# A graph layer on one core: the order of the edges is asked at the end of the program instead of by a branch at its beginning

## The chip, the cores and the metric

The kernel runs on one core of a Trainium2 chip. A core has a matrix engine (TensorE, "PE" in the profile; its weight loads are "PEld"), a vector engine (VectorE, "DVE"), a scalar engine (ScalarE, "ACT"), a general engine (GpSimd, "POOL") and a sync engine (SyncE, "SP") that here only issues transfers. Each engine works through its own queue in order. Transfers run on 16 DMA engines and are issued from the queues of SP, ACT and POOL. The metric is device time in microseconds (us), the median of several runs; lower is better.

## The reference

There are 6250 nodes with 256 numbers each (`x`) and 100000 edges `src -> dst`, which the inputs bring sorted by `dst`.

```python
theta_x = (x[dst] - x[src]) @ theta_w.T + theta_b
phi_x = x[src] @ phi_w.T + phi_b
e = relu(theta_x + phi_x)
out = segment_max(e, dst, num_segments=6250)      # 0 where a node has no edge
return layernorm(x + out)                          # eps 1e-5, no scale, no shift
```

Since `x[dst]` is the same for all edges of a node, the kernel takes the maximum over `b = x @ (phi_w - theta_w).T` of the source nodes first, and adds `x @ theta_w.T` and the biases of the node itself behind it.

## The kernel before

The program is one long list of instructions with no loop on the chip. It is written in program order; a scheduler then orders each engine's queue by when it reckons an instruction can start, program order first among those that are ready, so an instruction may be issued well ahead of its place in the text. Only the inside of a conditional block can't be mixed with what is outside it. The nodes are split: part 1 (the first 1130) is done from gathered rows alone, part 2 (the last 5120, 40 tiles of 128) mostly by selection matmuls.

**Beginning (L528 to L661).** SP loads `src_1`, ACT's queue loads `dst_i` and `dst_1` and copies both edge lists to `src_list` and `dst_list` in DRAM. L602 and L604 count the places where `dst` falls (`n_descents`), and `add_up` (L575: a matmul with ones and a copy) writes the count to `flags[0]`. `search_edges` (L621) finds for each partition where its window of 800 edges ends (`window`) and gathers that window (`dst_w`, `src_w`) on POOL. L652 loads the count into a register of every engine, and L653 branches: with a count over 0, a bitonic sort (`sort_edges`, L123) rewrites both lists, and the loads, the first gathers and the search are done again. With these inputs the count is 0 and the block is jumped over.

**Preparation (L710 to L784).** SP loads the weights (`w_in`, L719) and biases (L722); PE transposes the weights (L739). Twelve shares of up to four tiles of x (`x_q`, L775) and six groups of eight gathered rows (`x_group`, L764) are transposed by PE (L747), copied by ACT (L749), multiplied (L759) and copied out (L762); the shares go to `b_rows` in DRAM. The pools of this stage are closed at its end, and the tiles of the fetch stage below (`rows`, `raw`, `terms`, `want`, `hot`) are laid out behind that.

**Table and choice (L929 to L1031).** On DVE, `fill_table` spreads the window over a table of 40 nodes by 36 ranks (L938 to L979), and `choice` picks, for each of 17 blocks of source rows (slots), at most one edge per node (L1004 to L1022). `wanted` (L1024) transposes the choice and stores it to `chosen_rows`.

**Fetch (`slot_part`, L1056).** There are 85 parts: 17 slots by 5 blocks of 1024 nodes. A part loads its `want` row (L1061), builds three one-hot matrices (`hot`: two ACT passes each, L1067 and L1068; later the first by one DVE instruction, L1065), and PE multiplies them with the slot's rows in two terms (L1075, 24 matmuls). ACT copies the result of slot 0 (L1084), DVE takes the maximum for the others (L1086, twice per part). `terms` (L1053, L1054) are made once per slot.

**Runs of gathered rows.** POOL gathers rows with `gather` (L515; the DMA is issued in L512, and short `pause` instructions of L488 space the gathers out). DVE runs a capped maximum over them (L688), and SP stores them (L696). First 48 gathers of x, then 98 of `b_rows` (part 1), then the edges that no slot took: `list_pieces` (L1167 to L1235, DVE) compacts them, and 232 gathers by `list_src` fetch their rows (part 2). All POOL gathers are chained in program order (`in_turn`, L506).

**End (L1319 to L1344, L1454).** Shares of up to eight tiles: gather of the maxima (`place_1`, `place_2`), PE for `x @ theta_w.T`, DVE sum and ReLU, ACT for the variance (L1328) and the normalisation (L1338), store (L1344). Then all columns of `bad` (conditions under which the fast way does not hold) are added up, and L1461 branches to `general_path` if there was any; here it is jumped over.

Of the kernel before, what the change touches and what calls it, by code (L numbers as in the profile page):

```python
# [40 lines left out]
FP = mybir.dt.float32  # L41
# [6 lines left out]
ALU = mybir.AluOpType  # L48
# [4 lines left out]
P = 128  # L53
# [50 lines left out]
def load_rows(queue, t, src, total):  # L104

    n_rows, width = t.shape
    whole, rest = min(divmod(total, width), (n_rows, 0))
    queue.dma_start(t[:whole, :], flat(src, 0, [[width, whole], [1, width]]))
    if rest:
        queue.dma_start(t[whole : whole + 1, :rest], flat(src, whole * width, [[width, 1], [1, rest]]))  # L110


def load_chunks(queue, t, dst, steps, total):


    queue.dma_start(t[1 : P - 1, :], flat(dst, steps - 1, [[steps, P - 2], [1, steps + 2]]))
    queue.dma_start(t[0:1, 1:], flat(dst, 0, [[steps, 1], [1, steps + 1]]))
    first = (P - 1) * steps - 1
    n = min(total - first, steps + 2)
    queue.dma_start(t[P - 1 : P, :n], flat(dst, first, [[steps, 1], [1, n]]))  # L120


def sort_edges(nc, pool, psum, src, dst, src_sorted, dst_sorted, ident):  # L123

    n_edges = src.shape[0]
    width = 1 << (SORT_BITS - 7)
    n_blocks = width // P

    d = pool.tile([P, width], I32, name="sort_dst")
    s = pool.tile([P, width], I32, name="sort_src")
    nc.vector.memset(d, ID_MASK)
    nc.vector.memset(s, 0)
    load_rows(nc.sync, d, dst, n_edges)
    load_rows(nc.scalar, s, src, n_edges)


    index = pool.tile([P, width], I32, name="sort_index")
    nc.gpsimd.iota(index, pattern=[[1, width]], base=0, channel_multiplier=width)  # L140
    gray = pool.tile([P, width], I32, name="sort_gray")
    nc.vector.tensor_scalar(gray, index, 1, None, op0=ALU.logical_shift_right)
    nc.vector.tensor_tensor(gray, gray, index, op=ALU.bitwise_xor)

    keys = [pool.tile([P, width], FP, name=f"keys{i}") for i in range(2)]
    first = keys[0].bitcast(I32)
    nc.vector.tensor_scalar(d, d, ID_BITS, KEY_OFFSET, op0=ALU.logical_shift_left, op1=ALU.bitwise_or)
    nc.vector.tensor_tensor(first, d, s, op=ALU.bitwise_or)
    at = 0

    def compare(distance):
        nonlocal at
        a, b = (k.rearrange("p (a two b) -> p a two b", two=2, b=distance) for k in (keys[at], keys[1 - at]))
        nc.vector.tensor_tensor(b[:, :, 0, :], a[:, :, 0, :], a[:, :, 1, :], op=ALU.min)
        nc.vector.tensor_tensor(b[:, :, 1, :], a[:, :, 0, :], a[:, :, 1, :], op=ALU.max)
        at = 1 - at

    def transpose():

        nonlocal at  # L160
        ps = psum.tile([P, n_blocks, P], FP, name="sort_ps")
        for c in range(n_blocks):
            nc.tensor.transpose(ps[:, c, :], keys[at][:, c * P : (c + 1) * P], ident)
        nc.vector.tensor_copy(keys[1 - at], ps.rearrange("p c f -> p (c f)"))
        at = 1 - at

    flips = pool.tile([P, width], I32, name="sort_flips")
    for k in range(1, SORT_BITS + 1):
        bits, bit = (index, 1) if k == 1 else (gray, k - 1)
        nc.vector.tensor_scalar(  # L170
            flips, bits, 31 - bit, -(1 << 31), op0=ALU.logical_shift_left, op1=ALU.bitwise_and
        )
        now = keys[at].bitcast(I32)
        nc.vector.tensor_tensor(now, now, flips, op=ALU.bitwise_xor)
        j = k - 1
        if (1 << j) >= width:
            transpose()
            while (1 << j) >= width:
                compare((1 << j) // width)
                j -= 1  # L180
            transpose()
        while j >= 0:
            compare(1 << j)
            j -= 1

    done = keys[at].bitcast(I32)
    nc.vector.tensor_scalar(d, done, ID_BITS, ID_MASK, op0=ALU.logical_shift_right, op1=ALU.bitwise_and)
    nc.vector.tensor_scalar(s, done, ID_MASK, None, op0=ALU.bitwise_and)
    nc.sync.dma_start(flat(dst_sorted, 0, [[width, P], [1, width]]), d)
    nc.scalar.dma_start(flat(src_sorted, 0, [[width, P], [1, width]]), s)  # L190
# [237 lines left out]
def gnn_kernel(ctx: ExitStack, tc: tile.TileContext, x, src, dst, theta_w, theta_b, phi_w, phi_b, out):  # L428
# [106 lines left out]
    def gather_group(i, table, a=0, b=STEPS):  # L535
        t0, n = groups[i]
        if i not in ring_tiles:
            ring_tiles[i] = gathered.tile([P, STEPS, D], FP, name="g")
        return [
            gather(ring_tiles[i][:, k, :], table, src_1[:, t0 + k : t0 + k + 1]) for k in range(a, min(b, n))  # L540
        ]
# [33 lines left out]
    def add_up(per_partition, to):  # L575
        ps = misc()[0:1, 0:1]
        nc.tensor.matmul(ps, per_partition, ones, start=True, stop=True)
        nc.vector.tensor_copy(to, ps)
# [17 lines left out]
    nc.vector.memset(list_pads, PAD_WORD)  # L596
    nc.sync.dma_start(flat(list_words, 0, [[OWN_LIST, 1], [1, OWN_LIST]]), list_pads[:1, :])
    nc.sync.dma_start(flat(list_words, (P + 1) * OWN_LIST, [[OWN_LIST, 3], [1, OWN_LIST]]), list_pads[:3, :])
    bad = const.tile([P, 9], FP, name="bad")

    descents = search.tile([P, T + 1], FP, name="descents")
    nc.vector.tensor_tensor(descents, dst_i[:, : T + 1], dst_i[:, 1:], op=ALU.is_gt)  # L602
    n_descents = search.tile([P, 1], FP, name="n_descents")
    nc.vector.tensor_reduce(n_descents, descents, AX.X, ALU.add)  # L604
    add_up(n_descents, flags[:, 0:1])

# [12 lines left out]
    def search_edges():  # L621

        nc.vector.tensor_copy(ids[:, : T + 1], dst_i[:, 1:])
        iota(ids[:, T + 1 :], 0, 0, T)
        nc.vector.tensor_copy(low0, ids[:, 0:1])
        nc.vector.memset(low0[0:1, :], -1.0)
        nc.vector.tensor_scalar(last_node, first_node, TILES - 1.0, None, op0=ALU.add)
        nc.vector.tensor_scalar(hot0, columns[:, 2, :], low0, None, op0=ALU.is_ge)
        nc.vector.scalar_tensor_tensor(hot0, columns[:, 2, :], ids[:, T : T + 1], hot0, op0=ALU.is_lt, op1=ALU.mult)
        cut = 2 * D  # L630
        for i, (a, b, n) in enumerate(((cut, T + 2, T), (0, cut, cut))):
            pp = misc()
            nc.tensor.matmul(pp[:, : b - a], hot0, ids[:, a:b], start=True, stop=True)
            nc.vector.tensor_scalar(
                descents[:, a:n], pp[:, : n - a], last_node, None, op0=ALU.is_le, op1=ALU.add, accum_out=counts[:, i : i + 1]
            )
            nc.vector.tensor_tensor(end, counts[:, i : i + 1], end if i else pp[:, T + 1 - a : T + 2 - a], op=ALU.add)

        nc.vector.tensor_scalar(counts[:, 0:1], end, -float(WINDOW), 0.0, op0=ALU.add, op1=ALU.max)
        nc.vector.tensor_scalar(window, counts[:, 0:1], float(E - WINDOW), None, op0=ALU.min)  # L640
        nc.vector.tensor_scalar(bad[:, 0:1], end, float(WINDOW), None, op0=ALU.is_lt)
        gather_run(dst_w, dst_list, window)
        gather_run(src_w, src_list, window)

    search_edges()
    gather_group(of_x[0], x, EARLY_STEPS)

    with (
        tc.tile_pool(name="sort", bufs=1) as sort,
        tc.tile_pool(name="ps_sort", bufs=2, space=PSUM) as ps_sort,  # L650
    ):
        n_unsorted = nc.values_load(flags[0:1, 0:1])  # L652
        with tc.If(n_unsorted > 0):  # L653
            sort_edges(nc, sort, ps_sort, src, dst, src_list, dst_list, ident)
            load_chunks(nc.sync, dst_i, dst_list, T, EDGES)
            load_chunks(nc.sync, dst_1, dst_list, T1, EDGES)
            load_rows(nc.scalar, src_1, src_list, P * T1)
            latest[0] = None
            gather_group(of_x[0], x)
            search_edges()  # L660
    latest[0] = None  # L661
    early.close()
    for i in of_x[1:]:
        gather_group(i, x)
# [168 lines left out]
    def last_or_none(to, last_place, has, none):  # L833
        nc.vector.scalar_tensor_tensor(last_place, last_place, float(-none), has, op0=ALU.add, op1=ALU.mult)
        nc.vector.tensor_scalar(last_place, last_place, float(none), float(none), op0=ALU.add, op1=ALU.min)
        nc.vector.tensor_copy(to, last_place)

    def places_1():
        has = work.tile([P, NT1], FP, name="has_1")
# [615 lines left out]
    n_bad = const.tile([P, 1], FP, name="n_bad")  # L1455
    nc.vector.tensor_reduce(n_bad, bad, AX.X, ALU.add)
    add_up(n_bad, flags[:, 1:2])
    body.close()

    n_over = nc.values_load(flags[0:1, 1:2])  # L1460
    with tc.If(n_over > 0):  # L1461
        general_path(tc, x, theta_w, pick, bias_terms, out, b_rows, src_list, dst_list, ident, E)


# [22 lines left out]
```

## Time and profile before

| what | us |
| --- | --- |
| median of 3 runs | 749.13 (747.54 to 750.01) |
| the profiled execution | 746.02 |
| span of its instructions | 744.2 |
| PE busy | 650.4 (87%) |
| DVE busy | 641.4 (86%) |
| POOL busy | 604.9 (81%) |
| ACT busy | 492.7 (66%) |
| the 1960 matmuls of L1075 | 458.0 |

The page divides the span into 40 slices of 18.6 us and gives each engine's busy share in tenths; PEclk is the clock granted to TensorE, in the same tenths. Further views used are the list of waits (who waited for whom: total us, times, longest), the timeline (start us, duration us, engine, line, operation, and in brackets the idle time before it with what ended it), the stretches (busy time of each engine between two times) and the chain of waits that ended last.

### The profile page before, as it was taken

The page shows a single profiled execution, that of the slowest core. Times are in us where ns is not written, and L with a number is a line of the kernel's source. Part 1 is how long each engine was busy: PE and PEld are TensorE (multiplying, and loading weights), DVE is VectorE, ACT ScalarE, POOL GpSimd, SP SyncE. Part 2 cuts the span into 40 slices and gives each one's busy share as a digit, 9 for nine tenths or more (in the row PEclk, how much of TensorE's full clock was granted, in tenths as well). Part 3 has the DMA queues.
Part 4 walks back from the last instruction along what each step waited for, and adds up shares of the span by engine and source line. Part 5 has one row for each costly group of instructions (what it writes and reads, how often), then busy time and mean ns, then how long its engine had stood idle before and what let it go on. Part 6 is the DMA issues. An engine that isn't in the chain of part 4 may idle for free.

```text
span 744.2 us, 10255 instructions
## 1 busy us (share of the span) xinstructions
PE 650.4 (87%) x3018; PEld 537.3 (72%) x3018; DVE 641.4 (86%) x1197; ACT 492.7 (66%) x700; POOL 604.9 (81%) x843
## 2 busy tenths in 40 slices
PE   1299999939777999999999999999999999589970
PEld 0288888726556788688888888888888888479970
DVE  6699999999997989598889989889799899768871
ACT  0144444459997777688777877877787775037885
POOL 7788987788887778888888888888888888648840
PEclk9599999959999999999999999999999999999995
DMA  6577745584677787968777777768768777625542
GB/s 207 144 244 244 248 159 193 176 286 151 209 239 256 239 254 231 356 211 267 230 235 223 261 243 251 228 223 251 262 205 261 229 222 250 224 101 180 180 173 116
DMA packets 55895, 164.84 MB, mean 221 GB/s; under 512 B 11835, under 2 KB 19796, under 8 KB 48500
## 3 DMA queue, kind: packets, MB, share of 16 engines
q1 hardware_dynamic: 32344, 98.76, 38.1%
q0 software_dynamic: 20944, 57.62, 27.5%
q10 hardware_dynamic: 2540, 7.69, 2.9%
q8 instruction: 27, 0.44, 0.3%
q14 instruction: 40, 0.33, 0.1%
HBM read 101.08 MB, written 63.74 MB: 221 GB/s over the span
## 4 chain that ended last, share of the span: by engine, by line
PE 52%; ACT 11%; DVE 5%; DMA 5%; POOL 3%; issue 2%; DVEq 0%; ACTq 0%; POOLq 0%; SPq 0%
PE ps_f L1075 49%; DMA want<-chosen_rows 4%; POOL g L512 3%; ACT x_f L1338 3%; ACT squares L1328 3%; ACT hot L1067 2%; ACT hot L1068 2%; DVE acc L1086 2%; PE ps_e L1299 1%; ACT acc L1084 1%; DMA g<-b_rows,src 1%; ACT x_t L1294 1%; DVE g L688 1%; DVE x_f L1314 1%; DVE g L1310 0%
## 5 line engine op out<-in xcount | busy, mean ns | idle before, releaser
L1075 PE MATMUL ps_f<-hot,terms 128*128 128x512 f32 x1960 | 458.0, 395 | 29.0 <-ACT hot L1068 15.6
L1075 PEld LDWEIGHTS ps_f<-hot,terms 128*128 128x128 f32 x1960 | 370.2, 190 | 113.1 <-ACT hot L1068 19.8
L512 POOL DMA_INDIRECT g<-b_rows,list_src x232 | 235.4, 1015 | 39.4 <-issue 35.6
L1067 ACT ACTIVATE hot<-want,minus_row 128x1024 fp32r<-128x1024 f16 x169 | 186.2, 1147 | 92.7 <-PE ps_f L1075 80.2
L1086 DVE TENSOR_TENSOR acc<-acc,ps_f 128x1024 f32<-128x1024 f32 x160 | 193.5, 1215 | 31.9 <-PE ps_f L1075 31.0
L688 DVE SCALAR_TENSOR_TENSOR g<-g,caps 128x256 f32<-128x256 f32 x376 | 180.0, 479 | 8.4 <-DMA g<-b_rows,src 5.2
L1068 ACT ACTIVATE hot<-hot 128x1024 fp32r<-128x1024 f32 x169 | 169.1, 1046 | 0.0
L512 POOL DMA_INDIRECT g<-b_rows,src x98 | 128.0, 1306 | 30.5 <-issue 25.3
L488 POOL IOTA pause<- 128x160 f32 x384 | 120.4, 314 | 5.5
L759 PE MATMUL ps_b<-weights,x_t 128*128 128x256 f32 x388 | 90.5, 388 | 1.3 <-ACT x_t L749 0.5
L759 PEld LDWEIGHTS ps_b<-weights,x_t 128*128 128x128 f32 x388 | 72.9, 192 | 14.4 <-ACT x_t L749 5.0
L512 POOL DMA_INDIRECT g<-in_x_dram,src x48 | 60.3, 1256 | 11.3 <-issue 7.1
L512 POOL DMA_INDIRECT g<-maxima,place x49 | 47.6, 972 | 24.6 <-issue 22.5
L1065 DVE TENSOR_SCALAR hot<-want,row_id 128x1024 fp32r<-128x1024 f16 x76 | 59.8, 788 | 6.4 <-DMA want<-chosen_rows 6.3
L1299 PE MATMUL ps_e<-weights,x_t 128*128 128x256 f32 x192 | 48.5, 380 | 0.3 <-ACT x_t L1294 0.2
L1299 PEld LDWEIGHTS ps_e<-weights,x_t 128*128 128x128 f32 x192 | 32.8, 190 | 3.9 <-ACT x_t L1294 0.8
L1294 ACT COPY x_t<-ps_e 128x512 f32<-128x512 f32 x24 | 13.7, 574 | 32.4 <-PE ps_e L1292 32.4
L762 ACT COPY b_sb<-ps_b 128x512 f32<-128x512 f32 (+1 forms) x25 | 14.4, 578 | 29.8 <-PE ps_b L759 28.0
L762 ACT COPY g<-ps_b 128x512 f32<-128x512 f32 x24 | 14.1, 586 | 29.8 <-PE ps_b L759 27.5
L1338 ACT ACTIVATE x_f<-x_f,r 128x256 f32<-128x256 f32 x49 | 25.3, 590 | 10.8 <-DVE r L1335 10.7
L749 ACT COPY x_t<-ps_xt 128x512 f32<-128x512 f32 (+1 forms) x49 | 26.1, 593 | 0.0
L1328 ACT ACTIVATE squares<-x_f,r 128x256 bf16<-128x256 f32 x49 | 24.2, 499 | 1.6 <-DMA g<-b_rows,list_src 1.0
(266 smaller groups left out, 502.2 us busy)
## 6 DMA issues: line engine op xcount, KB each, us to landing
maxima<-g SPq DMA_DIRECT2D x47, 1024.0 KB
want<-chosen_rows SPq DMA_DIRECT2D x85, 256.0 KB
x_q<-in_x_dram SPq DMA_DIRECT2D x12, 512.0 KB
b_rows<-b_sb ACTq DMA_DIRECT2D x12, 512.0 KB
x_f<-in_x_dram SPq DMA_DIRECT2D x5, 1024.0 KB
out_dram<-x_f SPq DMA_DIRECT2D x5, 1024.0 KB
raw<-b_rows SPq DMA_DIRECT2D x16, 256.0 KB
g<-b_rows,list_src POOLq DMA_INDIRECT x232, 4.3
```

Of the source, the lines that this page charges most:

```text
L488: return nc.gpsimd.iota(t, pattern=[[step, t.shape[1]]], base=base, channel_multiplier=per_partition, allow_small_or_imprecise_dtypes=True,)
L512: in_turn(nc.gpsimd.indirect_dma_start(out=out, out_offset=out_offset, in_=in_, in_offset=in_offset))
L688: one = nc.vector.scalar_tensor_tensor(g[:, k, :], last[part], caps[:, t : t + 1], g[:, k, :], op0=ALU.min, op1=ALU.max)
L759: nc.tensor.matmul(ps[:, h, :], x_t[:, h, k, :], weights[:, k, 0, :], start=(k == 0), stop=(k == KC - 1))
L1065: nc.vector.tensor_scalar(hot[:, b, :], want, row_id[:, b : b + 1], None, op0=ALU.is_equal)
L1067: nc.scalar.activation(hot[:, b, :], want, AF.Abs, bias=minus_row[:, b : b + 1], scale=1.0)
L1068: nc.scalar.activation(hot[:, b, :], hot[:, b, :].bitcast(FP), AF.Relu, bias=1.0, scale=-1.0)
L1075: nc.tensor.matmul(ps[:, w : w + 512], terms[:, part, b, h * P : (h + 1) * P], hot[:, b, w : w + 512], start=(i == 0), stop=(i == n - 1),)
L1086: latest_part[0] = nc.vector.tensor_tensor(to, to, ps, op=ALU.max).ins.name
L1299: nc.tensor.matmul(a[:, i, :], x_t[:, 2 * i + c, :], weights[:, c, 1, :], start=(c == 0), stop=False)
L1328: nc.scalar.activation(squares, x_f[:, k, :], AF.Square, bias=mean[:, k : k + 1], scale=1.0, accum_out=var[:, k : k + 1])
L1338: nc.scalar.activation(x_f[:, k, :], x_f[:, k, :], AF.Identity, bias=mean[:, k : k + 1], scale=inv[:, k : k + 1])
```

## The change

The count of falls is no longer read at the beginning. It becomes a tenth column of `bad`, so that unsorted edges lead into the conditional block at the end, and `flags[0]` is written there. The sort stands inside that block, in an inner conditional of its own, ahead of the general path, which then runs on the sorted lists. The repeated loads, gathers and search fall away. Because the fast way now also runs over unsorted edges, one place index is kept from falling below 0.

```diff
-    bad = const.tile([P, 9], FP, name="bad")
+    bad = const.tile([P, 10], FP, name="bad")
...
-    n_descents = search.tile([P, 1], FP, name="n_descents")
+    n_descents = bad[:, 9:10]
     nc.vector.tensor_reduce(n_descents, descents, AX.X, ALU.add)
-    add_up(n_descents, flags[:, 0:1])
...
     search_edges()
     gather_group(of_x[0], x, EARLY_STEPS)
-
-    with (
-        tc.tile_pool(name="sort", bufs=1) as sort,
-        tc.tile_pool(name="ps_sort", bufs=2, space=PSUM) as ps_sort,
-    ):
-        n_unsorted = nc.values_load(flags[0:1, 0:1])
-        with tc.If(n_unsorted > 0):
-            sort_edges(nc, sort, ps_sort, src, dst, src_list, dst_list, ident)
-            load_chunks(nc.sync, dst_i, dst_list, T, EDGES)
-            load_chunks(nc.sync, dst_1, dst_list, T1, EDGES)
-            load_rows(nc.scalar, src_1, src_list, P * T1)
-            latest[0] = None
-            gather_group(of_x[0], x)
-            search_edges()
-    latest[0] = None
     early.close()
...
-        nc.vector.tensor_copy(to, last_place)
+        nc.vector.tensor_scalar(to, last_place, 0.0, None, op0=ALU.max)
...
     add_up(n_bad, flags[:, 1:2])
+    add_up(n_descents, flags[:, 0:1])
     body.close()
 
     n_over = nc.values_load(flags[0:1, 1:2])
     with tc.If(n_over > 0):
+        n_unsorted = nc.values_load(flags[0:1, 0:1])
+        with (
+            tc.tile_pool(name="sort", bufs=1) as sort,
+            tc.tile_pool(name="ps_sort", bufs=2, space=PSUM) as ps_sort,
+            tc.If(n_unsorted > 0),
+        ):
+            sort_edges(nc, sort, ps_sort, src, dst, src_list, dst_list, ident)
         general_path(tc, x, theta_w, pick, bias_terms, out, b_rows, src_list, dst_list, ident, E)
```

## The prediction

> **What bounds the kernel now.** I read the 40 slices first, then the chain, then the stretches and waits at both ends of it.
>
> ```profile
> PE   1299999939777999999999999999999999589970
> DVE  6699999999997989598889989889799899768871
> ```
>
> PE stands still in the first 30 us and works with gaps from slice 9 to 14 (about 150 to 280 us). DVE is full from slice 3 on.
>
> ```profile
> 150.00:200.00 50.00, 33.69 (x121) 24.68 (x121) 48.99 (x85) 41.21 (x67) 43.12 (x28) 0.80 0.68 219
> 400.00:500.00 100.00, 100.00 (x442) 82.79 (x442) 89.44 (x130) 77.86 (x78) 88.94 (x133) 1.00 0.75 238
> 311.66 309.57 PE ps_f L1075 x1364
> ```
>
> The first two lines are stretches (busy us, with counts in brackets, of PE, PEld, DVE, ACT, POOL; granted clock; DMA), the third is the chain's longest piece. From 311 us to 621 us PE is busy without a break on the fetch matmuls, so every microsecond of fetch done before that comes off the end, if nothing else holds the end. What else holds it is POOL:
>
> ```profile
> 277.18 1.14 POOL L512 DMA_INDIRECT g<-b_rows,list_src  x1 [1.79 <-DVE caps L1235]
> 660.81 0.95 POOL L512 DMA_INDIRECT g<-maxima,place  x1 [15.07 <-issue]
> ```
>
> POOL gathers from 277 us to 645.5 us with no idle time but about 0.2 us of issue per gather, then waits 15.07 us for the last maxima to be stored. So the end has two supports: PE's fetch, and POOL with 15.07 us to spare.
>
> **The beginning.**
>
> ```profile
> PE ps_xt L739 <- DMA biases<-in_L_gnn_phi_b_dram: 15.4, 1, 15.4
> DVE ids L669 <- DVEq L653: 4.0, 1, 4.0
> POOL g L512 <- DMA src_w<-src_list,window: 2.5, 1, 2.5
> SPq L719 <- POOLq L653: 3.5, 1, 3.5
> ...
> L653 SPq COMPARE_BRANCH  x1: 45/45/45, 10.2 to 10.2; - x1
> L653 POOLq COMPARE_BRANCH  x1: 53/53/53, 24.5 to 24.5; - x1
> ...
> 25.02 0.39 SPq L719 DMA_DIRECT2D w_in<-in_L_gnn_phi_w_dram  x1
> 34.23 2.65 PE L747 MATMUL ps_xt<-ident,x_q 128*128 128x128 f32 x10
> ```
>
> SP is at the branch at 10.2 us, POOL, behind its gathers, only at 24.5 us; SP's load of the weights waits for that and goes out at 25.02 us. PE transposes the first x tile at 34.23 us, although the first x tiles were asked for at 3.75 us. The weights wait and the x tiles don't, presumably because w_in's place is one that a sort tile had. A third place shows where the preparation's end is waited for:
>
> ```profile
> 148.16 0.26 ACT L1030 CAST rows<-ps 80x128 f16<-80x128 f32 x1
> 161.94 2.19 ACT L1067 ACTIVATE hot<-want,minus_row 128x1024 fp32r<-128x1024 f16 x2
> ```
>
> The first choice was transposed by PE at 95.75 us, but is copied out only at 148.16 us, right behind the last copy of the preparation (147.68 us), whose space it takes over; the first one-hot follows at 161.94 us.
>
> **The change, part by part.**
>
> (1) *Weights.* Without the branch SP can issue w_in where it now issues x_q (3.75 us) or before it. Landing took 5.8 us (25.02 to 30.8). From 4 to 14 us the DMA engines are 0.83 to 1.02 busy at about 300 GB/s, so the 0.77 MB of weights and biases cost some 2.6 us there. 3.75 + 5.8 + 2.6 = 12.1, plus 3.4 us for the weight transposes (30.8 to 34.2): x at about 15 us. If the weights go out first, at about 1 us, it is 10 us; with a slip of 2 to 3 us on SP's queue, 17. I take 14, which is 20 us earlier, between 17 and 24. The same 0.77 MB could delay the window's lists by 0 to 2.6 us; I take 0, since the DMA engines are only 0.02 busy at 16 to 18 us, before the window is gathered at 18.01 us.
>
> (2) *Preparation.* From 36 to 100 us PE is over 98% busy, so it is its own limit and ends 20 us earlier, at 128 us. It needs the x gathers: POOL's last is issued at 109.6 us, the change takes 2.5 us off (4), and a gather lands in 3.9 us, so they are there at 111; the last group takes PE 7 us, from 121. They don't hold it.
>
> (3) *Fetch begins.* The 14.3 us from 147.68 to 161.94 (clearing raw, slot loads, want) I keep. ACT is then the limit (25.00 of 25 us in 200 to 225). This stretch shifts by the 20 us.
>
> (4) *POOL.* The branch cost POOL the 2.5 us of idle time above. The list gathers at 277.18 us had waited 1.79 us for DVE; DVE's list work comes earlier (5), so they start at 277.2 - 2.5 - 1.8 = 272.9, 4.3 us earlier. At the end POOL could then go on 15.07 + 4.3 = 19 us earlier: the most that this support allows.
>
> (5) *DVE.* It idles from 17.7 to 25.8 us but for 0.24 us. Fifteen groups of small work on weights, biases and caps now lie behind 25.8 us in the table's way: by their rows 0.16 + 0.22 + 0.68 + 0.42 + 0.27 + 0.41 + 0.44 + 0.47 + 4 x 0.41 for L726 to L740 and 1.6 for L673 to L806 make 6.3 us. They can move into that idle time. So choice and list work end about 6 us earlier, 0 to 6.3.
>
> (6) *How much of PE's 20 us stays.* A part that is not of slot 0 costs DVE 2 x 1.21 + 0.75 = 3.2 us and PE 24 x 0.234 = 5.6 us. DVE is full from 150 to 225 us, so parts done earlier need DVE time: the 6.3 us, and 7.9 us idle from 225 to 277 (44.12 of 52.00 busy), of which 5.2 us are waits for gathers (L688) and may stay. 6.3 + 2.7 = 9.0 us give 2.8 parts, 16 us of PE; all 14.2 us give 4.4 parts, 25 us. Slot 0's five parts are copied by ACT, so the low end is safer than it looks. I take 16, the case where the gather waits stay, between 6 and 20.
>
> (7) *The end.* The second add_up is two passes of 0.19 us in all on PE and 0.14 us on DVE (L577, L578), at about 635 us, where PE waits 2.6 us for a one-hot; uncovered, 0.35 us. The extra max takes the copy's place (L836, 0.17 us; its neighbour L835, two operations, 0.38): 0.2 us, before a 1.03 us wait of DVE; uncovered, 0.2. What the branch jumps over gets longer; there it is the same jump, and the trace bounds it: DVE's branch is at 736.6 us and its next event at 739.4, so -0 to +2.8 us; I take 0, since the target was not near before either. Five loads of the count (0.5 us each) and five branches vanish inside (1) and (4).
>
> On (7), the Trainium skill (Runtime: NRT & Kernel Launch, Instruction fetch mechanics) says that a taken branch to a target outside the window loaded must first fetch the target's page; by that rule a longer block costs the same one fetch, so 0, and if every jump cost a second fetch, the sum would be 736 instead of 733. The trace's 3.1 us on DVE at L653 (18.2 to 21.3) agrees with a fetch.
>
> Sum: PE 16, POOL 19, the smaller counts. 744.2 - 16 = 728; with 1.8 us around the span 730 against 746.0 for that execution. This lies 3.1 us under the median of 749.13, so in the metric I forecast **733 us**.
>
> **The rivals.**
>
> *A, the forecast: fetch moves ahead.* 12 to 20 us off: 729 to 737. For it: PE's idle start, its full stretch, POOL's 15 us. Chance 0.50.
>
> *B, DVE or POOL holds the lead back.* DVE's order stays as it is, parts gain only its 6.3 us, or the end follows POOL's 4.3 us because its last wait is not free: 743 to 745. For it: DVE's 48.99 of 50; against it: L1086 can fill DVE's waits. Chance 0.24. The Trainium skill (SBUF — State Buffer, Who interferes with whom) lets a DVE operation in a two-port mode shut POOL out altogether. By it the 0.75 us of L1065 for 4.4 earlier parts would cost POOL 3.3 us, leaving POOL 15.7 and the sum near 733; the gathers of 206 to 276 us, with L1065 among them, take 1.08 us against 0.95 at best, so the trace shows little of it.
>
> *C, more than forecast:* the 14.3 us of (3) shrink too, and POOL's 19 us or more come off: 725 to 729. Chance 0.08.
>
> *D, it doesn't do what it says:* another dependence still keeps the weights back, only POOL's 2.5 us go: 747 to 749. Against it: the row names L653. Chance 0.07.
>
> *E, slower.* The earlier fetch puts L1086 and L1054 ahead of the list work in DVE's queue, and the list gathers, behind which POOL has an unbroken row to 645 us, start later. Each part ahead costs 3.2 us, less the 6.3. It decides once they start later than 277 + 15 = 292, that is from seven parts on ((15.07 + 6.3) / 3.2). With all nine parts that the choice loop holds: 9 x 3.2 - 6.3 - 15.1 = 7.4 us lost, 756. For it: those parts come first in program order; against it: ACT needs 6.6 us for a part's three one-hots, so only three or four fit into the 20 us. Chance 0.11.
>
> **How the numbers follow.** A, B and C are faster by over 0.3% (2.2 us, about what a measurement can tell from no change): 0.82. D is 0.07 the same, E 0.11 slower. The predicted time is A's. The range leaves out D, E and the extremes of C: 725 to 746.
>
> **What would show it.** Weights issued by SP before 10 us and x transposed by 17; the last copy of L762 at about 128 instead of 147.68; the first L1067 at about 142; choice (L1022) and L1235 some 6 us earlier; the first list gather at about 273; PE unbroken from before 311; the wait before the last gathers (15.07) down to a few us. Wrong it would be if L1075 starts early but the list gathers start after 277 (E), or if the weights go out late (D).

## The result and the profile after

The kernel after took 752.26 us (median of 20 runs, 749.96 to 757.0) against 749.21 for the one before (20 runs, 743.11 to 755.5): ratio 1.0054, 95% interval 1.0032 to 1.0076. A later pair of measurements gave 752.03 against 750.18, ratio 1.0031 (0.9997 to 1.0065). The profiled span went from 744.2 to 751.2 us. But the profiled execution of before (746.02) was 3.2 us faster than the median of its runs, and that of after (752.98) 0.7 us slower: 3.9 of these 7.0 us are scatter of single executions, and the medians differ by 3.05. The forecast was 733, so the change came out on the other side.

From L653 on, a line of before has a number lower by 16 in after (L688 is now L672). The slices of PE and DVE after:

```profile
PE   1999999277379799989999999999999999589980
DVE  6499999997799979779979889889889899768881
```

PE does start early now, in the second slice, and has a new hole in the eighth (131 to 150 us). DVE has a seven in five slices between the 10th and the 20th (10, 11, 15, 17, 18); before it had one seven (13) and one five (17) there. The stretches (busy us and counts of PE, PEld, DVE, ACT, POOL; granted clock; DMA), of after:

```profile
125.00:150.00 25.00, 11.68 (x54) 8.86 (x52) 24.19 (x62) 6.64 (x21) 19.81 (x18) 0.77 0.66 219
150.00:200.00 50.00, 35.38 (x135) 26.00 (x133) 43.17 (x92) 48.28 (x69) 41.29 (x33) 0.87 0.71 235
200.00:250.00 50.00, 33.82 (x133) 26.30 (x134) 45.28 (x77) 36.07 (x52) 41.30 (x31) 0.84 0.62 195
```

and of before, the two that were not shown:

```profile
125.00:150.00 25.00, 22.13 (x115) 18.62 (x113) 24.41 (x64) 11.19 (x22) 19.95 (x17) 1.00 0.60 202
200.00:250.00 50.00, 39.04 (x161) 29.36 (x161) 44.37 (x94) 43.25 (x66) 39.64 (x35) 0.97 0.78 246
```

Up to 125 us PE was busy 107.5 us after and 95.4 before: a lead of 12.1 us. In 125 to 150 it loses 10.5 of it and in 200 to 250 another 5.2, where it also runs at a granted clock of 0.84 instead of 0.97. DVE did 5.8 us less work in 150 to 200 (43.17 against 48.99). From 400 to 500 us PE is busy throughout in both (100.00 us).

Waiting is only a part of what PE lost. The page's rows for the fetch matmuls (busy us, mean ns of one; then the idle time before them), of before and of after:

```profile
L1075 PE MATMUL ps_f<-hot,terms 128*128 128x512 f32 x1960 | 458.0, 395 | 29.0 <-ACT hot L1068 15.6
L1059 PE MATMUL ps_f<-hot,terms 128*128 128x512 f32 x1960 | 464.0, 398 | 39.5 <-DVE hot L1049 13.4
```

The same 1960 matmuls take 6.0 us more. Most take 0.39 us; 29 of them took over 0.6 us in before and 53 in after, and these stand in groups behind PE's waits, where the granted clock is low (0.50 from 139 to 162 us in after). From the start to the end of the last fetch matmul, all 2602 matmuls together kept PE busy 583.2 us in before and 587.2 in after, and PE stood idle for 69.4 and 72.6 us. So of the 7.2 us by which the last fetch matmul came later, 4.0 are longer busy time (the fetch matmuls 6.0 more, the others 2.0 less) and 3.2 are added waiting.

Now the beginning, in after's waits of the first 35 us (us in total, times, longest):

```profile
POOL dst_w L512 <- DVE window L639: 7.8, 1, 7.8
PE ps_xt L723 <- DVE weights L724: 6.4, 1, 6.4
DVE w_in L718 <- DMA w_in<-in_L_gnn_theta_w_dram: 2.5, 1, 2.5
DVE ids L653 <- DMA dst<-in_dst_dram: 2.4, 1, 2.4
DVE bias L710 <- DMA biases<-in_L_gnn_phi_b_dram: 2.1, 1, 2.1
```

and the same in the order of time, SP, DVE, PE and POOL (start, us, instruction, idle time before it and its releaser):

```profile
1.19 0.42 SPq L703 DMA_DIRECT2D w_in<-in_L_gnn_phi_w_dram  x1
6.97 0.69 DVE L718 TENSOR_TENSOR w_in<-w_in 128x512 f32<-128x512 f32 x1 [2.50 <-DMA w_in<-in_L_gnn_theta_w_dram]
...
13.13 1.72 DVE L711 CAST high_part<-bias 128x256 fp32r<-128x256 f32 x1
...
24.91 0.15 DVE L639 TENSOR_SCALAR window<-counts 128x1 int32<-128x1 f32 x1
17.71 1.20 PE L731 MATMUL ps_xt<-ident,x_q 128*128 128x128 f32 x3 [1.26 <-DVE weights L724]
25.33 0.96 POOL L512 DMA_INDIRECT dst_w<-dst_list,window  x1 [7.83 <-DVE window L639]
```

The weights go out at 1.19 us and x is transposed at 17.71. But weights, biases and the chunk ids now stand *in front of the search* in DVE's queue, and DVE stands still for each of their loads; the window is ready at 24.91 us instead of 17.59. The middle and the end, on ACT and POOL:

```profile
135.25 0.26 ACT L1014 CAST rows<-ps 80x128 f16<-80x128 f32 x1
153.49 1.16 ACT L1051 ACTIVATE hot<-want,minus_row 128x1024 fp32r<-128x1024 f16 x1
...
287.21 1.02 POOL L512 DMA_INDIRECT g<-b_rows,list_src  x1 [0.30 <-issue]
667.96 0.95 POOL L512 DMA_INDIRECT g<-maxima,place  x1 [11.43 <-issue]
```

The preparation ends 12.9 us earlier (135.25 against 148.16), the fetch begins 8.5 us earlier (153.49 against 161.94), and the list gathers start 10 us *later* (287.21 against 277.18). Between the first two lies this, on DVE:

```profile
143.12 0.40 DVE L988 TENSOR_SCALAR wide<-padded 128x960 int16<-128x960 int16 x1
143.63 0.70 DVE L1019 MEMSET raw<- 128x768 f32 x1
144.25 0.36 DVE L672 SCALAR_TENSOR_TENSOR g<-g,caps 128x256 f32<-128x256 f32 x1
144.53 0.27 DVE L806 TENSOR_SCALAR hot<-columns,low 128x128 f32<-128x128 f32 x1
...
168.84 0.65 DVE L1006 TENSOR_TENSOR unused<-unused,wide 128x960 int16<-128x960 int16 x1
...
189.73 0.49 DVE L672 SCALAR_TENSOR_TENSOR g<-g,caps 128x256 f32<-128x256 f32 x1 [4.41 <-DMA g<-b_rows,src]
```

Line 988 begins a new round of the choice, and it is broken off: raw's memset and node_place's one-hots (L806), with runs (L672) between them, come first. Before, the same instructions stood behind the whole choice, whose last instruction is L1022:

```profile
149.70 0.66 DVE L1022 TENSOR_TENSOR unused<-unused,wide 128x960 int16<-128x960 int16 x1
...
152.55 0.70 DVE L1035 MEMSET raw<- 128x768 f32 x1
```

Before, the choice ended at 150.36 us. After, it ends at 169.49 (L1006), and the runs have got so far ahead (79 by 170 us, 62 before) that they wait for the rows that POOL gathers: 9.8 us in 150 to 260, against 5.2 before. What comes behind them in DVE's queue waits too: PE had to wait 8.1 us for one slot's terms (L1038).

### The profile page after: what moved, and what is told of

Same layout as the page of the kernel before. It is cut to its first block, busy times and chain, and to the rows that moved or that the text cites. A ratio compares the mean times of both kernels' runs of the same rounds, so it can differ in the third digit from the quotient of the medians.

```text
span 751.2 us, 10220 instructions
## 1 busy us (share of the span) xinstructions
PE 654.4 (87%) x3018; PEld 539.9 (72%) x3018; DVE 639.7 (85%) x1197; ACT 493.1 (66%) x700; POOL 606.7 (81%) x843
## 4 chain that ended last, share of the span: by engine, by line
PE 40%; DVE 12%; DMA 9%; POOL 8%; ACT 8%; issue 4%; DVEq 0%; SPq 0%; ACTq 0%; POOLq 0%
PE ps_f L1059 37%; POOL g L512 6%; DMA want<-chosen_rows 4%; ACT x_f L1322 3%; DVE acc L1070 3%; DMA g<-b_rows,src 3%; ACT squares L1312 3%; DVE g L672 2%; PE ps_e L1283 1%; POOL pause L488 1%; DMA g<-b_rows,list_src 1%; ACT hot L1051 1%; DVE work L1187 1%; DMA raw<-b_rows 1%; DVE hot L1049 1%
## 5 line engine op out<-in xcount | busy, mean ns | idle before, releaser
L1059 PE MATMUL ps_f<-hot,terms 128*128 128x512 f32 x1960 | 464.0, 398 | 39.5 <-DVE hot L1049 13.4
L672 DVE SCALAR_TENSOR_TENSOR g<-g,caps 128x256 f32<-128x256 f32 x376 | 180.2, 479 | 12.8 <-DMA g<-b_rows,src 9.8
L1052 ACT ACTIVATE hot<-hot 128x1024 fp32r<-128x1024 f32 x169 | 169.0, 1046 | 0.0
L512 POOL DMA_INDIRECT g<-in_x_dram,src x48 | 61.9, 1289 | 9.1 <-issue 7.1
L1322 ACT ACTIVATE x_f<-x_f,r 128x256 f32<-128x256 f32 x49 | 25.3, 589 | 10.6 <-DVE r L1319 10.5
```

Of the source, the lines that this page charges most:

```text
L512: in_turn(nc.gpsimd.indirect_dma_start(out=out, out_offset=out_offset, in_=in_, in_offset=in_offset))
L672: one = nc.vector.scalar_tensor_tensor(g[:, k, :], last[part], caps[:, t : t + 1], g[:, k, :], op0=ALU.min, op1=ALU.max)
L1052: nc.scalar.activation(hot[:, b, :], hot[:, b, :].bitcast(FP), AF.Relu, bias=1.0, scale=-1.0)
L1059: nc.tensor.matmul(ps[:, w : w + 512], terms[:, part, b, h * P : (h + 1) * P], hot[:, b, w : w + 512], start=(i == 0), stop=(i == n - 1),)
L1322: nc.scalar.activation(x_f[:, k, :], x_f[:, k, :], AF.Identity, bias=mean[:, k : k + 1], scale=inv[:, k : k + 1])
```

## The experiments

Three theories stood against each other. *B*: the window, 7.3 us late, is carried to the end. *M2*: the loss is DVE's order in the middle. *P*: the end is set by PE's fetch, and the list gathers matter little. Besides these, *M* says only that the earlier preparation is to blame, *N* that it is the code moved to the end or the missing branch.

The chips differed. On three of five (marked s; the other two are called quiet) the kernels stood still at several places, for up to 26.6 us at once. From the last fetch matmul to the end of the span the profiles there show 118 to 122 us, where the quiet ones of the table show 91.0 to 91.6, and before took 816 to 825 us there instead of 749 to 753. Such a stop in the first run of hold_weights, as the profile's waits show it:

```profile
DVE acc L1081 <- remote: 29.0, 4, 26.6
```

There times are compared only with before on the same chip, and what the trace tells is read ahead of the first long stop; in before_shift1, hold_shift1 and raw_apart_2 shorter ones, of up to 4.8 us, lie ahead of what is read.

| kernel | ratio to before (95%) | window | preparation ends | choice ends | first list gather | last fetch matmul | span |
|---|---|---|---|---|---|---|---|
| before | 1 | 17.6 | 148.3 | 150.4 | 277.2 | 652.6 | 744.2 |
| after | 1.0054 (1.0032 to 1.0076) | 24.9 | 135.3 | 169.5 | 287.2 | 659.8 | 751.2 |
| after_again | 1.0031 (0.9997 to 1.0065) | 25.1 | 134.6 | 169.0 | 286.8 | 657.6 | 749.0 |
| hold_weights_3 | 1.0057 (1.0019 to 1.0095) | 18.0 | 148.0 | 149.5 | 287.3 | 664.2 | 755.3 |
| search_first_3 | 1.0003 (0.9977 to 1.0029) | 16.6 | 145.7 | 163.2 | 279.3 | 659.0 | 750.0 |
| choice_ahead_2 | 0.9993 (0.9964 to 1.0021) | 25.4 | 133.7 | 157.8 | 281.7 | 655.0 | 746.4 |
| choice_search_2 | 0.9989 (0.9957 to 1.0021) | 16.6 | 147.1 | 153.0 | 282.5 | 658.2 | 749.5 |

Starts and ends in us, each from the one profiled execution of its kernel. The two profiles of after differ by 0.8 us at most up to the first list gather, but by 2.2 us at the last fetch matmul. The profiles also come from different chips, and some lie well off their kernel's median: before's 3.2 us under it, choice_ahead_2's 3.4 us. So a few microseconds in the last two columns decide nothing; the ratios do, and of these the last four are from one chip, on which after itself was not timed.

**after_again**, no edit.

> The kernel after, unchanged, on the chip of the study, beside before. If the loss is the same there as at first: ratio 1.003 to 1.008, window at 25 us, last copy of the preparation at 135, choice ended at 169, first list gather at 287. If the chip's state adds stalls that neither kernel had at first, the ratio may lie anywhere between 0.98 and 1.02; then only the stretches ahead of the first such stall are compared between kernels.

As expected; a quiet chip.

**hold_weights, hold_weights_2, hold_weights_3**: the change without its earlier preparation. The load of w_in waits for the window's gather, and SP's other loads of the preparation stand behind it.

```diff
+                tc.add_manual_dep(load.ins, window_read[0], landed, reason="after the window")
...
+            behind_in_order(one, held, "after the window")
```

> The kernel after, with the loads of w_in, biases and x_q held behind the landing of the window's dst_w gather: no branch, but the preparation starts when it did with the branch. Theory M (all of the loss comes from the preparation being earlier): the window at about 17.6 us, the last copy of the preparation at 145 to 148, choice ended by 152, the first list gather at 275 to 279, the last fetch matmul at 650 to 654, ratio to before 0.994 to 1.001. Rival N (the work put at the end, or the branch's absence itself, costs the 4 us): the middle is back as said, but the ratio stays at 1.003 to 1.010, and the stretch behind the last fetch matmul is longer than before's 92 us.

> The kernel of hold_weights once more: no branch, the preparation as late as before. Theory M (the earlier preparation causes the loss): window at 17 us, choice ended by 151, first list gather at 272 to 279, last fetch matmul 648 to 654, ratio 0.992 to 1.001. Theory N (the work at the end, or the code without the branch, costs it): the middle as before, ratio 1.003 to 1.010.

> The kernel of hold_weights again, on a chip without the stalls of the earlier two looks. Theory M (the earlier preparation causes the loss): window at 17 us, choice ended by 151, last COPY_PREDICATED at 213 to 226, first list gather at 272 to 280, last fetch matmul 648 to 654, ratio 0.992 to 1.001. Theory N (the work at the end, or the code without the branch, costs it): the middle as before, ratio 1.003 to 1.010.

The runs on s chips gave 1.0064 (1.0017 to 1.0112) and 0.9970 (0.9868 to 1.0073), the quiet one 1.0057. N's first half falls: from the last fetch matmul to the end of the span it is 91.0 us here, 91.4 in after, 91.6 in before, so the code moved to the end costs nothing. M falls as the only cause: window, preparation and choice are where before has them, and yet the list gathers come at 287 us and the kernel is slow. N's other half, that the missing branch alone costs something by another way, is not excluded: this kernel has no branch either, its beginning is where before has it, and it is slow. POOL's gathers (start, us) in hold_weights_3:

```profile
180.33 7.69 POOL L512 DMA_INDIRECT g<-b_rows,src  x1 [0.30 <-issue]
188.32 9.49 POOL L512 DMA_INDIRECT g<-b_rows,src  x1 [0.30 <-issue]
...
202.57 7.41 POOL L512 DMA_INDIRECT g<-b_rows,src  x1 [0.30 <-issue]
```

and in before, at the same place:

```profile
179.85 3.75 POOL L512 DMA_INDIRECT g<-b_rows,src  x1 [0.30 <-DMA g<-b_rows,src]
183.91 3.02 POOL L512 DMA_INDIRECT g<-b_rows,src  x1 [0.30 <-issue]
187.24 2.25 POOL L512 DMA_INDIRECT g<-b_rows,src  x1 [0.30 <-issue]
```

At 210 us hold_weights_3 has issued 46 of these gathers, before 54, and the runs use the rows up:

```profile
DVE g L675 <- DMA g<-b_rows,src: 15.5, 10, 3.5
```

That is three times before's 5.2 us in 150 to 260. So the middle of the kernel before is near an edge: a little less speed of the gathers there, and DVE waits.

**search_first, search_first_2, search_first_3**: DVE's work on weights, biases and chunk ids stands behind the window.

```diff
+    one = nc.vector.tensor_copy(ids_1[:, : T1 + 2], dst_1)
+    behind_in_order(one, found[0], "the window first")
...
+        one = nc.vector.tensor_sub(w_in[:, 0], w_in[:, 0], w_in[:, 1])
+        behind_in_order(one, found[0], "the window first")
```

> The kernel after, with VectorE's work on weights and biases, and the copy of ids_1, placed behind the instruction that makes the window; everything else stays early. Theory B (the 7.3 us by which the window came late at the begin are carried to the end): the window back at 17 to 19 us, the table's end 5 to 6 us earlier than after's 87.8, the first list gather at 281 to 284 instead of 288.7, ratio to before 0.995 to 1.000. Theory M2 (the middle: VectorE's order there, with raw's memset, node_place and runs ahead of the last rounds of the choice, and its waits for GpSimd's rows): the table's end moves, but the choice's last instruction stays at 162 or later, the list gathers at 285 or later, ratio 1.001 to 1.007.

> The kernel of search_first once more: the window back at 17 us, weights still early. Theory B (the late window is carried to the end): first list gather at 281 to 284, ratio 0.995 to 1.000. Theory M2 (VectorE's order in the middle): the choice's last instruction at 162 or later, list gathers at 285 or later, ratio 1.001 to 1.007.

> The kernel of search_first again, on a chip without the stalls. Theory B (the late window is carried to the end): choice ended at 160 to 164, first list gather at 280 to 283, ratio 0.995 to 1.000. Theory M2 (VectorE's order in the middle): the choice's last instruction at 162 or later, list gathers at 285 or later, ratio 1.001 to 1.007.

With stops 1.0017 (0.9960 to 1.0074) and 0.9775 (0.9690 to 0.9860), quiet 1.0003. The list gathers come at 279.3, just ahead of B's range (280 to 283) and against M2 (285 or later). The last fetch matmul reads 659.0, as in after, while the ratio is that of before. This chip's before has a median of 753.1, 4 us above the one of the first measurement, so the single profile does not tell whether the end followed the list gathers, and P stays undecided here. The preparation, though its x is transposed at 27.2 us and not 34.2, ends only 2.5 us earlier than before's: PE waits 10.0 us for w_in's subtraction and later 4.1 us for a round of the choice whose transposition now lies ahead of its own.

**list_first, both_first**: choice and list pieces have first place wherever the scheduler may choose; both_first with search_first's edit.

```diff
+        with tc.high_priority():
+            choice(s0)
+            wanted(s0)
...
+        with tc.high_priority():
+            if next(pieces, pieces) is pieces:
```

> The kernel after, with the choice, wanted and the pieces of the list given first place wherever the scheduler has a choice; the begin stays as in after (the window at 25 us). Theory M2: the choice ends by 160 instead of 168.8, the last COPY_PREDICATED by 225 instead of 261, the first list gather at 255 to 278 instead of 288.7, ratio to before 0.985 to 0.998. Theory B: VectorE's total decides, the list gathers move by less than 4 us, ratio 1.002 to 1.008. Third theory P (TensorE's row sets the end, and it is the matmuls of the fetch done by 250 us that count): the list gathers come 10 us or more earlier, but the last fetch matmul stays at 656 or later and the ratio at 1.000 to 1.012, since parts are put off for the list.

> Both edits, search and list first. Theories B and M2 together: window at 18, table's end at 82, choice ended by 153, first list gather at 250 to 272, ratio 0.975 to 0.992. Theory P: the list gathers as early, but the last fetch matmul not before 652 and the ratio 0.996 to 1.008.

Both s. list_first 1.035 (1.0246 to 1.0453); both_first 846.64 against 815.75 us, medians, with no interval. The preparation ended at 172 us and the choice at 186 and 176. Stops lie ahead of that in both traces, so these two only show that this was no way out.

**choice_ahead, choice_ahead_2**: raw's memset and node_place's first DVE instruction stand behind the choice's last.

```diff
+    for one in put_off:
+        behind_in_order(one, choice_end[0].ins.name, "the choice first")
```

> The kernel after, in which only the memset of raw and the first VectorE instruction of each node_place are placed behind the choice's last instruction on VectorE; the begin stays as in after (window at 25 us). Theory M2: the choice ends at 156 to 162 instead of 169, but the first hot waits for it (from 153 to 165 or later); the list gathers at 275 to 283 instead of 287; ratio 0.996 to 1.003. Theory B: the list gathers stay within 3 us of 287 and the ratio at 1.003 to 1.009. Theory P (TensorE's fetch sets the end): the list gathers come earlier, the last fetch matmul stays at 657 to 664 and the ratio at 1.002 to 1.010.

> The kernel of choice_ahead again, on a chip without the stalls. Theory M2: the choice ended at 156 to 160, last COPY_PREDICATED at 222 to 238 instead of 261, first list gather at 275 to 283 instead of 287, ratio 0.994 to 1.002. Theory B: list gathers within 3 us of 287, ratio 1.003 to 1.009. Theory P (TensorE's fetch sets the end): list gathers earlier, but the last fetch matmul at 656 or later and the ratio 1.002 to 1.010.

s: 0.9786 (0.9679 to 0.9893); quiet: 0.9993, an interval that does not meet after's first one (1.0032 to 1.0076) but does meet its second (0.9997 to 1.0065). The choice ends at 157.8, the last COPY_PREDICATED at 238.2 instead of 261.6, the list gathers at 281.7, each in M2's range or at its edge, and the ratio is in it too. P's forecast, a ratio of 1.002 to 1.010 with the last fetch matmul at 656 or later, missed. So DVE's order in the middle is enough to explain what after lost; no more than that comes back.

**choice_search, choice_search_2**: both edits.

> Both edits: the search ahead of the weights' work, and the choice ahead of raw's memset and of node_place. The order in the middle is before's, with everything ahead of it some 8 us earlier. Theory M2 with B: choice ended by 151, first hot at 150 to 158, list gathers at 268 to 275, last fetch matmul at 640 to 648, ratio 0.980 to 0.995. Theory P alone, with list and fetch apart: list gathers at 268 to 277, last fetch matmul at 648 to 656, ratio 0.995 to 1.003.

> The kernel of choice_search again, on a chip without the stalls. Theories M2 and B together: choice ended by 154, first hot at 152 to 157, list gathers at 268 to 276, last fetch matmul at 640 to 650, ratio 0.980 to 0.997. Theory P: list gathers at 268 to 277, last fetch matmul at 650 to 657, ratio 0.997 to 1.004.

s: 0.9855 (0.9779 to 0.9932); quiet: 0.9989. Window, choice and first hot (155.3) are in range, the list gathers (282.5) and the last fetch matmul (658.2) are later than either theory said; the ratio is in P's range (0.997 to 1.004) and not in the other's. Behind the choice DVE waits 12.4 us for gathered rows, one gather taking 8.8 us. The two gains do not add up.

**hold_shift1, before_shift1**: one memset of 0.1 us more ahead of the list pieces.

```diff
+        shifted = work.tile([P, 1], FP, name="shifted", bufs=1)
+        nc.vector.memset(shifted, 0.0)
```

> The kernel of hold_weights with one memset of a 128x1 tile more on VectorE ahead of the pieces of the list (some 0.1 us; else the same order on VectorE but for one run). Theory G (GpSimd's gathers are held up while VectorE runs the list's shifts and predicated copies, and for how long depends on how the two engines' instructions happen to meet): the three gathers of 7.7, 9.5 and 7.4 us between 180 and 210 us become others, the sum of gathers over 3.3 us there changes by 5 us or more either way, and the first list gather moves by 3 us or more from 287. Rival G2 (these gathers wait for something fixed, their rows or a ring of descriptors): the same three long gathers within 1 us, the first list gather at 286 to 289, ratio 1.002 to 1.009.

> The kernel before with the same one memset ahead of the pieces of the list, and the order of VectorE that the scheduler makes of it (predicated copies behind node_place instead of ahead of it in four places). Theory G: before's middle (no gather over 3.8 us) was a fortunate meeting; one or more gathers of 5 us and over appear between 180 and 215 us, the first list gather comes at 280 to 290 instead of 277, ratio 1.001 to 1.010. Rival: nothing changes, gathers under 4 us, first list gather at 276 to 279, ratio 0.997 to 1.002.

Both s; hold_shift1 816.38 against 818.8 us (medians), before_shift1 1.0111 (0.9975 to 1.0248). hold_shift1 has gathers of 7.7, 9.4 and 6.3 us where hold_weights_3 has 7.7, 9.5 and 7.4, and before_shift1 none over 4.3. So the long gathers neither came nor went with a shift of a tenth of a microsecond, against what theory G forecast. In both traces the preparation already ends later than in the quiet ones (153.6 us against 148.0, and 160.4 against 148.3), so the first list gather says nothing here. What makes the gathers long in the one kernel and not in the other stays open.

**raw_apart, raw_apart_2, raw_apart_search**: raw has memory of its own and is cleared at the begin (before, it takes over the preparation's memory and must wait for it); node_place stands behind the choice; the third with search_first's edit.

```diff
+    raw = const.tile([P, KB, D], FP, name="raw")
+    nc.vector.memset(raw, LOWEST)
```

> The kernel after, with the tile raw in memory of its own (its memset early, not behind the preparation whose memory it had) and node_place behind the choice's last instruction. Theory P (TensorE's idle time between the preparation and the fetch is what the early preparation wasted): first fetch matmul at 140 to 150 instead of 156.7, TensorE busy 18 us or more in 125 to 150 instead of 11.7, last fetch matmul at 640 to 652, ratio 0.980 to 0.996. Theory M2 alone (VectorE's row decides): the fetch starts earlier but its parts wait for VectorE, last fetch matmul at 652 to 658, ratio 0.996 to 1.004.

> The kernel of raw_apart again, for a chip without stalls (in the look with stalls the first fetch matmul came at 154.9 us, 1.8 earlier than in after, and the first list gather at 293). Theory P: first fetch matmul at 150 to 155, last fetch matmul at 645 to 653, ratio 0.988 to 0.998. Theory M2 alone: the list gathers at 281 to 287, last fetch matmul at 653 to 659, ratio 0.998 to 1.005.

> raw_apart with the search ahead of the weights' work as in search_first. Theory P with B: first fetch matmul at 148 to 157, list gathers at 270 to 280, last fetch matmul at 642 to 653, ratio 0.982 to 0.997. Theory M2 alone: 0.996 to 1.003.

All s: 0.9899 (0.9753 to 1.0046), 0.9726 (0.9608 to 0.9844) and 1.0111 (0.9990 to 1.0233). The first fetch matmul came at 154.9 us in raw_apart and in raw_apart_2, only 1.8 us earlier than in after, and at 160.6 in raw_apart_search, behind the forecast's 148 to 157. SP's queue and ACT in raw_apart_2 show why:

```profile
144.54 0.32 SPq L682 DMA_DIRECT2D maxima<-g  x1
144.91 1.57 SPq L1048 DMA_DIRECT2D want<-chosen_rows  x2
...
151.68 2.19 ACT L1054 ACTIVATE hot<-want,minus_row 128x1024 fp32r<-128x1024 f16 x2 [12.47 <-DMA want<-chosen_rows]
```

The first load of want stands in SP's queue behind a store of maxima, which waits for a group of runs on DVE until 144.54 us; then the load takes 6.8 us to land. So raw's memset was one thing that held the begin of the fetch, and SP's order the next. Whether this kernel is faster than before on a quiet chip was not measured. No version here is shown to beat the one before on a quiet chip.

## Why the prediction was wrong

The step that failed is (5), and (6) on top of it: "So choice and list work end about 6 us earlier", and with that DVE time "I take 16". Both took DVE's order as given and moved work within it. But the order is made anew by the scheduler from what is ready when. With the preparation's end 13 us earlier, raw's memset and node_place were ready before the choice was through and went in ahead of it. The choice ended 19 us later instead of 6 earlier, and the list gathers started 10 us later; putting these instructions back (choice_ahead_2) brought the choice's end to 157.8 us and the time level with before. (6) also had no term for PE's clock: of the 7.2 us by which the last fetch matmul came later, 4.0 are time that the same matmuls kept PE busy longer.

Point by point:

(1) *Weights*: issued at 1.19 us, and x transposed at 17.71, 0.7 us behind the late end of the forecast's 10 to 17. The price was looked for in the wrong place: "I take 0" for the window's lists, because the DMA engines are free there. It was not the DMA engines but DVE's queue, where 2.5, 2.1 and 2.4 us of waiting came to stand ahead of the search, and the window was 7.3 us late. search_first_3 removes this waiting and comes out level with before, so it is worth about as much as the middle; the two do not add.

(2) *Preparation*: ended 12.9 us earlier, not 20. Of the 7.1 us that are missing, 3.5 are x's later start (PE waits 6.4 us for the weights' copies on DVE); the rest was not traced.

(3) *Fetch begins*: the gap that was kept at 14.3 us became 18.7 (134.76, the start of the last copy, to 153.49). It was taken as one stretch, though it begins with a DVE instruction, raw's memset, which after came 8.4 us behind the preparation's end instead of 4.4, and holds a load behind SP's stores.

(4) *POOL* and the end: the list gathers came 10 us later instead of 4.3 earlier, and the 15.07 us of POOL's wait became 11.43. In the seven quiet profiles of the table this wait is 10.5 to 18.7 us, and in all seven the gathers behind it start 7.8 to 8.2 us behind the last fetch matmul. So PE alone set the end in each of them; the 19 us of POOL's limit were never reached, and whether it would hold the end there is not shown. E's threshold of 292 us was not reached either: the kernel became slower with the list gathers at 287. E was right in its sign and its place (work put ahead of the list on DVE), wrong in the work (raw's memset, node_place and runs, not the fetch's L1086 and L1054) and in the condition.

(6) *PE's lead*: 12.1 us at 125 us, then 14.6 us less than before's work from 125 to 300 (130.3 us busy against 144.9), with a granted clock of 0.87 there instead of 0.93; the last fetch matmul came 7.2 us later, and the span grew by 7.0, both between two single executions.

(7) *The end* at 0 was right: 91.4 us behind the last fetch matmul against 91.6.

Shown: that undoing either cause alone brings the time level with before (0.9993 and 1.0003, where after has 1.0054 and 1.0031), and the end's innocence. Shown by the traces alone: that matmuls at a lower granted clock are a part of the loss; after_again has the same (587.0 us busy and 70.6 idle up to the last fetch matmul). Not shown: that the two causes are the whole loss, since hold_weights_3 has neither of them, only its long gathers, and stays at 1.0057. Open: the long gathers, and why undoing both causes gives no more than undoing one.

## What to carry over

A barrier that is taken out at the begin changes the order of every queue behind it, so each engine's new order has to be read, not the old one shifted: ask of each instruction that becomes ready earlier whose turn it will take. If a long wait near the end always ends the same time behind another engine's last instruction, that other engine sets the end, and starting the waiting engine's work earlier does not move it. And where a stage lives on rows gathered just in time, an earlier begin of their user can turn into waiting: here the runs were 17 ahead at 170 us and then waited 9.8 us instead of 5.2.

## What the runs showed of the hardware

DVE and POOL seem to hold each other up more than the profile before let one expect. In after the cast of L711 took 1.72 us and the TENSOR_SCALAR of L713 1.70, where before the same two took 0.27 and 0.44. The cast ended at 14.85, just behind POOL's iota of 1440 elements (13.36 to 14.70 us); in choice_ahead_2, where that iota was over before the cast began, the cast took 0.29. The Trainium skill (SBUF — State Buffer, Who interferes with whom) says that casts and tensor_scalar in a two-port mode and GpSimd shut each other out for a whole instruction; these two rows agree with it, though no run shows in which mode the two instructions ran.

In the other direction POOL's gathers, 0.95 us each at best and 1.02 in the mean of the 232 list gathers, took 2.0 us in the mean from 160 to 215 us in before (46.5 us for 23), where DVE does the list's shifts and predicated copies, and up to 9.5 in hold_weights_3. By the rule of the Trainium skill (SBUF — State Buffer, Who interferes with whom) one lock lasts one DVE instruction, and the longest beside the three long gathers is 1.87 us, so a gather of 9.5 us would need several in a row; the runs don't show which, nor that DVE is the cause.

On three of five chips the engines stopped, for up to 26.6 us, and before took 9% longer. In the first two runs of hold_weights, on two such chips, DVE's longest stop ended at 270 and at 272 us; no run here shows the cause.
